# Transposes by halves of rows, VectorE's statistics behind the first projection, and band copies shared between ScalarE and VectorE

## The chip, the cores and the metric

The kernel runs on one core of a Trainium2 chip. The metric is the device time of one execution in microseconds, given as the median of the runs shown. TensorE multiplies and transposes into PSUM, which has eight banks of 512 fp32 columns in this kernel's use. VectorE and ScalarE empty PSUM, GpSimd (POOL in the profile) works in SBUF, and SyncE's queue (SP) issues nearly all DMAs.

## The reference

Two layers of the same form work on an image `x` of 512 x 512 positions with 64 channels. `_gn` normalises `x` over groups of two channels and all positions. Then, with DIM 64, HID 128 and WIN 4:

```python
xn = _ln(x, norm_scale, norm_bias)
left  = (xn @ Wl + bl) * mask * sigmoid(xn @ Wlg + blg)
right = (xn @ Wr + br) * mask * sigmoid(xn @ Wrg + brg)
out_gate = sigmoid(xn @ Wog + bog)
out = _banded_ingoing(left, right, WIN)   # out[i, j] = sum over k, |k - i| <= 4, of left[k, i] * right[k, j]
out = _ln(out, out_norm_scale, out_norm_bias) * out_gate
return out @ Wo + bo
# x = x + layer0(_gn(x)); x = x + layer1(_gn(x))
```

Everything is fp32. The band sum is, for each hidden channel, a product of a banded matrix of `left` with `right`.

## The kernel before

Rows of the image are cut into nine overlapping blocks of 64. Columns are taken in two halves of 256, and both halves lie above one another on the 128 partitions: partitions 0 to 63 hold the block's rows for columns of the first half, 64 to 127 the same rows for the second. A **unit** is 8 columns of both halves (`JU = 8`), 128 x 512 numbers; 16 units make a **chunk** of 128 columns, and each layer has 18 chunks, so 288 units and 288 outputs.

The work is staged over steps `t` in `layer`, and every instruction inside it keeps the order in which it is written (`InOrder`, line 355; the trace puts all of them at line 362). One step works on several units of different age:

- `load`, then `affine` on GpSimd (the group normalisation: `z` times `ga`, plus `gb`), `inner_stats` on VectorE (`sti`), and `inner_norm` on GpSimd (`z` minus mean, times `rs`).
- `transposed` (line 430): four TensorE transposes of 128 x 128 from `z` into one bank, one ScalarE instruction into `zT`, and a DMA of `zT` to `later`.
- `right` (line 459), twice per unit: four products into a pair of banks, a sigmoid on ScalarE into `sg`, and a product on VectorE into `RO`. `left` is alike and runs only in the first few steps.
- `mix` (line 511): sixteen products of the band matrix `A` with `RO` into a pair of banks, copied back to `RO` by halves. A chunk's 16 mixes lie in ten of 16 steps: 2, 1, 2, 2, 1, 2, 1, 2, 2, 1; the other six have none.
- `out_stats` on VectorE (`sto`), `norm` on ScalarE (eight instructions into `on`), both on mixed columns.
- `recall` fetches `zT` again as `zg`; `gates` (line 594) multiplies it by the gate weights and takes the sigmoid into `gate`; `turned` (line 613) transposes `on` into two banks, and VectorE multiplies each by its gate into `ZH`.
- `fetch` loads the old `x` into `XR`, `biased` adds a bias on GpSimd, `end` multiplies `ZH` by `Wo`, adds on VectorE, and stores. In the first layer `sums` gathers the next group normalisation's sums on TensorE.
- `solve`, every fourth step: a few VectorE instructions (`var`, `nm`, `rs`) and the inverse square root on GpSimd for four steps' statistics.

On TensorE a step runs: gates, right, right, transposes of `z`, `turned`, `end`, `sums`, mixes. Outputs run 30 steps behind the units; between them lie the first steps without outputs, and at the end of a layer steps without units.

PSUM is dealt out by two pools: `one_bank` (three buffers in the first layer, where `acc` takes the eighth bank, four in the second) and `two_banks` (two buffers of a pair). A buffer is given again only when all its readers are done. `right` and `mix` take pairs; gates, transposes and `end` take single banks.

The copies of `mix` are shared so:

```python
            if on_scalar[n]:
                en.scalar.copy(o, v)
            else:
                en.vector.tensor_copy(o, v)
...
                mix(c, A[c, h0 // HA], h0, [True, n + 1 < len(mixes[t])])
```

so that of a step's last mix the first half goes to ScalarE and the second to VectorE, and of an earlier one in that step both halves go to ScalarE.

Of the kernel before, what the change touches and what calls it, by code (L numbers as in the profile page):

```python
# [8 lines left out]
F32 = mybir.dt.float32  # L9
I32 = mybir.dt.int32  # L10
AF = mybir.ActivationFunctionType
ALU = mybir.AluOpType
# [67 lines left out]
def tile_two_banded_layers(  # L80
# [47 lines left out]
    def one_bank():  # L128
        return ps.tile([P, 512], F32, tag="ps", name="bank")
# [290 lines left out]
    def inner_stats(u: Unit, st: bass.AP, k: int):  # L420

        en.vector.bn_stats(st[:, k, :], u.z[:, 2 * k : 2 * k + 2, :].rearrange("p t c -> p c t"))
# [6 lines left out]

    def transposed(u: Unit):  # L430

        u.t = ztp.tile([P, JU // 2, P], F32, tag="zT", name="zT")
        pt = one_bank()
        for k in range(JU // 2):
            en.tensor.transpose(
                pt[:, k * P : (k + 1) * P],
                u.z[:, 2 * k : 2 * k + 2, :].rearrange("p j c -> p (j c)"), ident,
            )
        en.scalar.activation(u.t.rearrange("c k p -> c (k p)"), pt, AF.Identity, bias=1.0)
        if u.near is None:  # L440
            en.sync.dma_start(later[u.at], u.t)

    def place(k: int, e: int) -> int:

        return k // 2 * 4 + 2 * e + k % 2
# [62 lines left out]
            )  # L508
        return A

    def mix(c: int, A: bass.AP, h0: int, on_scalar: list):


        j0 = c % 2 * (JC - JW)
        R = RO[:, :, j0 : j0 + JC, :]
        pb = two_banks()
        ph = pb.rearrange("i (h j) -> i h j", j=JC)
        for turn in range(2):
            for h in range(HB // 2):
                for e in range(2):  # L520
                    part = slice(e * S, (e + 1) * S)
                    hh = (turn ^ e) * (HB // 2) + h
                    en.tensor.matmul(
                        ph[part, hh, :], lhsT=A[part, :, h0 % HA + hh],
                        rhs=R[part, (h0 + hh) // 2, :, hh % 2],
                        start=True, stop=True,
                    )
        q = HB // 4
        for n in range(2):
            o = R[:, h0 // 2 + n * q : h0 // 2 + (n + 1) * q]  # L530
            v = pb.rearrange("i (h t j) -> i h j t", t=2, j=JC)[:, n * q : (n + 1) * q]
            if on_scalar[n]:
                en.scalar.copy(o, v)
            else:
                en.vector.tensor_copy(o, v)
# [54 lines left out]
    def recall(o: Out):  # L590
        o.t = ztg.tile([P, JU // 2, P], F32, tag="zg", name="zg")
        en.sync.dma_start(o.t, later[o.at])

    def gates(o: Out, w: dict):
        b = o.blk
        o.g = []
        pgs = [
            one_bank()[:, : 2 * JQ * b.m].rearrange("h (k p) -> h k p", p=b.m) for e in range(2)
        ]
        for e, pg in enumerate(pgs):  # L600
            part = slice(e * D, (e + 1) * D)
            en.tensor.matmul(
                pg, lhsT=w["gate"][part],
                rhs=o.t[part].rearrange("c k (e p) -> c (k e) p", e=2)[:, :, b.lo : b.hi],
                start=True, stop=True,
            )
        for pg in pgs:
            g = gp.tile([H, 2 * JQ * (S - WIN)], F32, tag="gate", name="gate")
            g = g[:, : 2 * JQ * b.m].rearrange("h (k p) -> h k p", p=b.m)
            en.scalar.activation(g, pg, AF.Sigmoid)  # L610
            o.g.append(g)

    def turned(o: Out, w: dict):

        b = o.blk
        for e in range(2):
            pt = one_bank()
            for k in range(JQ):
                en.tensor.transpose(
                    pt[:, k * P : (k + 1) * P], o.on[:, place(k, e), :], ident  # L620
                )
            zh = ZH[(2 * o.n + e) % len(ZH)]
            en.vector.scalar_tensor_tensor(
                zh[:, :, : b.m], pt.rearrange("h (k p) -> h k p", p=S)[:, :, b.lo : b.hi], w["ob"], o.g[e],
                ALU.add, ALU.mult,
            )

    def rows_of(v: bass.AP, o: Out, e: int):
# [14 lines left out]
    def end(dst: bass.AP, o: Out, w: dict):  # L643
        m = o.blk.m
        po = one_bank().rearrange("i (j c) -> i j c", c=D)
        for k in range(JQ):
            for e in range(2):
                for n in range(2):

                    en.tensor.matmul(  # L650
                        po[n * S : (n + 1) * S, 2 * k + e, :],
                        lhsT=ZH[(2 * o.n + e) % len(ZH)][:, 2 * k + n, :], rhs=w["Wo"],
                        start=True, stop=True,
                    )
        f = o.xr[: S + m, :, 1 : 1 + 2 * D]
        en.vector.tensor_tensor(
            f, po[: S + m].rearrange("i (k t) c -> i k (t c)", t=2), f, ALU.add
        )
        for e in range(2):
            en.sync.dma_start(rows_of(dst, o, e), o.xr[e * S : e * S + m, :, 1 : 1 + 2 * D])  # L660
# [13 lines left out]
    def layer(src: bass.AP, dst: bass.AP, w: dict, stats: bool, then=None):  # L674
# [56 lines left out]
        for t in range(min(loads), last_t + 3):  # L731
            if then and t == max(units) + 2:
                then()
            for u in loads.get(t, []):
                if u not in early:
                    load(src, u)
            if t + 2 in outs:
                recall(outs[t + 2])
            if t + 1 in outs:
                fetch(src, outs[t + 1], w, t + 1)  # L740
            for c, h in slabs.get(t, []):
                A[c, h] = take_left(c // per, h)

            for o in looks.get(t, []):
                if sto is None:
                    sto = sm.tile([P, NB // 2, 6], F32, tag="sto", name="sto"), []
                st, os = sto
                for k in range(JU // 2):
                    out_stats(o, st[:, len(os) * (JU // 2) :], k)
                os.append(o)  # L750

            for u in affines.pop(t, []):
                affine(u, en.vector if u.at < NU + 4 else en.gpsimd)
            if t % 4 == 3 and t > NU:
                then_affine = affines.pop(t + 1, [])
            if t in outs:
                gates(outs[t], w)

            todo = []
            for at, u in inners.get(t, []):  # L760
                key = (at + 2) // 4
                if key not in sti:
                    sti[key] = sm.tile([P, 3 * NB // 4, 6], F32, tag="sti", name="sti", bufs=3), []
                st, us = sti[key]
                n = len(us) * (JU // 2)
                u.mean = st[:, n : n + JU // 2, 1::3]
                todo += [(u, st[:, n : n + JU // 2, :], k) for k in range(JU // 2)]
                us.append(u)
            for v in todo[: len(todo) // 2]:
                inner_stats(*v)  # L770
            if t in units:
                for q in range(0, JU, JQ):
                    right(units[t], q, w)
            if t in lefts:
                for q in range(0, min(JU, NEAR * JQ - lefts[t].near), JQ):
                    left(lefts[t], q, w)
            for u in inputs(t + 2):
                inner_norm(u)
            for u in inputs(t + 1):
                transposed(u)  # L780
            if t in outs:
                turned(outs[t], w)
                biased(outs[t], w, stats)
            for v in todo[len(todo) // 2 :]:
                inner_stats(*v)
            if t - 1 in outs:
                end(dst, outs[t - 1], w)
            if stats and t - 2 in outs:
                sums(outs[t - 2], t - 2 == first_t, t - 2 == last_t)
            if t % 4 == 3:  # L790
                st, us = sti.pop((t + 5) // 4, (None, []))
                so, os = sto or (None, [])
                sto = None
                for u in then_affine:
                    affine(u, en.gpsimd)
                then_affine = []
                if us or os:
                    solve(w, us, os, st, so)
            if t + 1 in outs:
                norm(outs[t + 1])  # L800
            for n, (c, h0) in enumerate(mixes.get(t, [])):
                mix(c, A[c, h0 // HA], h0, [True, n + 1 < len(mixes[t])])

    class Slices:

# [84 lines left out]
    lp = ctx.enter_context(tc.tile_pool(name="lp", bufs=NA))  # L890
    wk = ctx.enter_context(tc.tile_pool(name="wk", bufs=3))
    onp = ctx.enter_context(tc.tile_pool(name="onp", bufs=1))
    gp = ctx.enter_context(tc.tile_pool(name="gp", bufs=2))

    next(one, None)
    nc.sync.dma_start(pack, spare)
# [35 lines left out]
```

## Time and profile before

| | |
|---|---|
| Median of 3 runs | 5073.46 us (5070.14 to 5074.28) |
| The profiled execution's own time | 5074.14 us, span 5072.3 us |
| TensorE matmul busy | 4496.1 us, 89% of the span |
| GpSimd, ScalarE, VectorE busy | 3826.9, 3793.8, 3732.8 us |
| Granted TensorE clock | 0.978 over the span, 1.0 in the steady stretches |
| One chunk of 16 steps, steady | 124.9 us (first layer), 121.1 us (second) |

Busy time is the union of an engine's instructions; idle time of an engine that nobody waits for costs nothing. In the timeline each line is a run of like instructions on one engine: start, length, engine, operation, `out<-in`, sizes and count; a bracket tells the idle time ahead of it and what ended it. fp32 products appear in the trace as two instructions each, transposes as one. The last row of the table is taken from the starts of the gate products in the trace.

### The profile page before, as it was taken

To read this page: it belongs to the slowest core of one execution; us is meant where nothing else is said; L and a number is where in the kernel's file an instruction comes from. 1 tells how busy PE (TensorE), PEld (TensorE's weight loads), DVE (VectorE), ACT (ScalarE), POOL (GpSimd) and SP (SyncE) were. 2 spreads that over 40 slices of the span, in tenths; PEclk is the share of its full clock that TensorE was granted. 3 is DMA by queue.
4 is the path that set the end of the run, shared out by engine and by line. 5 is a ranking of instruction groups with operands and counts; after the bars stand their busy time and mean duration, and the time that the engine had idled before them with its cause. 6 is when DMAs were issued, how large, how long until landed. Compare 5 with 4: busy or idle time off the path is not lost.

```text
span 5072.3 us, 159784 instructions
## 1 busy us (share of the span) xinstructions
PE 4496.1 (89%) x60138; PEld 3714.8 (73%) x60138; DVE 3732.8 (74%) x9445; ACT 3793.8 (75%) x8328; POOL 3826.9 (75%) x4739
## 2 busy tenths in 40 slices
PE   1027999999999999999995599999999999999999
PEld 0015788888888888888873478888888888888886
DVE  6764677777777777777766467777777777777776
ACT  0013788888888888888884268888888888888888
POOL 0037888888888888888733598888888888888863
PEclk9988999999999999999997799999999999999999
DMA  7924666666666666666663456767676776777766
GB/s 317 400 58 125 176 194 197 195 195 193 198 196 195 194 194 197 196 194 198 189 171 102 106 176 201 202 198 202 200 205 201 202 203 200 202 204 204 204 182 173
DMA packets 905291, 981.45 MB, mean 193 GB/s; under 512 B 114210, under 2 KB 641608, under 8 KB 900168
## 3 DMA queue, kind: packets, MB, share of 16 engines
q1 hardware_dynamic: 897248, 948.49, 63.5%
q10 hardware_dynamic: 7272, 22.73, 1.1%
q8 instruction: 477, 7.82, 0.7%
q14 instruction: 294, 2.41, 0.2%
HBM read 658.42 MB, written 312.46 MB: 191 GB/s over the span
## 4 chain that ended last, share of the span: by engine, by line
PE 72%; POOL 9%; DMA 6%; DVE 4%; ACT 3%; issue 2%; SPq 2%; another core or an unknown queue 0%; ACTq 0%; POOLq 0%; DVEq 0%
PE banks L362 38%; PE bank L362 32%; POOL z L362 6%; ACT on L362 2%; DMA left_of<-nothing 2%; PE acc L362 2%; SPq L362 2%; DVE RO L362 1%; POOL XR L362 1%; DMA gn_x<-in_x_dram 1%; POOL rsqrt L362 1%; DVE ZH L362 1%; DMA XR<-mid_x 1%; DVE sto L362 1%; ACT gate L362 1%
## 5 line engine op out<-in xcount | busy, mean ns | idle before, releaser
L362 ACT ACTIVATE on<-RO,nm,rs 128x128 f32<-128x128 f32 x4608 | 1879.2, 495 | 172.4 <-PE bank L362 169.9
L362 PE MATMUL banks<-pack,zT 64*128 64x256 f32 x9360 | 1213.1, 389 | 137.0 <-ACT zT L362 76.6
L362 PEld LDWEIGHTS banks<-pack,zT 64*128 64x128 f32 x9360 | 967.2, 192 | 419.8 <-issue 180.4
L362 PE MATMUL banks<-RO,A 64*64 64x128 f32 x18432 | 1154.5, 277 | 15.6 <-DVE RO L362 15.4
L362 PEld LDWEIGHTS banks<-RO,A 64*64 64x64 f32 x18432 | 1082.4, 183 | 43.6 <-DVE RO L362 18.6
L362 DVE TENSOR_TENSOR RO<-banks,sg 128x512 f32<-128x512 f32 x1152 | 747.0, 681 | 258.8 <-ACT sg L362 258.0
L362 ACT ACTIVATE sg<-banks 128x512 f32<-128x512 f32 (+1 forms) x1188 | 682.7, 589 | 319.8 <-PE banks L362 208.0
L362 DVE COPY RO<-banks 128x512 f32<-128x512 f32 x360 | 248.9, 692 | 869.1 <-ACT RO L362 869.1
L362 DVE BATCH_NORM_STATS2 sto<-RO 128x6 f32<-128x256 f32 x2304 | 797.5, 411 | 1.2
L362 DVE SCALAR_TENSOR_TENSOR ZH<-bank,pack,gate 128x448 f32<-128x448 f32 (+1 forms) x1152 | 740.0, 682 | 37.6 <-ACT gate L362 36.3
L362 POOL TENSOR_TENSOR z<-z,gb 128x512 f32<-128x512 f32 x536 | 687.7, 1283 | 42.1
L362 POOL TENSOR_TENSOR z<-z,ga 128x512 f32<-128x512 f32 x536 | 687.5, 1283 | 0.1
L362 PE MATMUL bank<-zg,pack 64*128 64x448 f32 (+1 forms) x2304 | 657.4, 595 | 18.9 <-DVE ZH L362 15.8
L362 PE MATMUL bank<-pack,ZH 128*64 128x64 f32 x18432 | 663.5, 225 | 2.8 <-ACT zT L362 0.3
L362 ACT ACTIVATE gate<-bank 128x448 f32<-128x448 f32 (+1 forms) x1152 | 567.1, 542 | 126.6 <-PE bank L362 125.8
L362 PEld LDWEIGHTS bank<-pack,ZH 128*64 128x64 f32 x18432 | 584.0, 138 | 100.3 <-ACT zT L362 83.2
L362 POOL TENSOR_TENSOR z<-z,rs 128x512 f32<-128x512 f32 x586 | 618.0, 1055 | 45.9
L362 PE MATMUL bank<-ident,on 128*128 128x128 f32 x4608 | 616.6, 274 | 14.7 <-ACT gate L362 12.1
L362 POOL TENSOR_TENSOR z<-z,sti 128x512 f32<-128x512 f32 x586 | 623.8, 1065 | 0.0
L362 ACT COPY RO<-banks 128x512 f32<-128x512 f32 x792 | 441.2, 586 | 239.0 <-PE banks L362 237.8
L362 PEld LDWEIGHTS bank<-ident,on 128*128 128x128 f32 x4608 | 519.7, 141 | 74.0 <-ACT on L362 24.3
L362 POOL TENSOR_TENSOR XR<-XR,pack 120x512 f32<-120x512 f32 (+1 forms) x352 | 418.4, 1189 | 192.4 <-DMA XR<-mid_x 90.4
(137 smaller groups left out, 3927.6 us busy)
## 6 DMA issues: line engine op xcount, KB each, us to landing
later<-zT SPq DMA_DIRECT2D x576, 256.0 KB
A<-left_of SPq DMA_DIRECT2D x576, 256.0 KB
zg<-later SPq DMA_DIRECT2D x576, 256.0 KB
z<-in_x_dram SPq DMA_DIRECT2D x576, 128.0 KB
z<-mid_x SPq DMA_DIRECT2D x576, 128.0 KB
gn_x<-in_x_dram SPq DMA_DIRECT2D x16, 4096.0 KB
XR<-in_x_dram SPq DMA_DIRECT2D x448, 112.0 KB
mid_x<-XR SPq DMA_DIRECT2D x448, 112.0 KB
```

Of the source, the lines that this page charges most:

```text
L362: return lambda *a, **k: tc.keep_in_program_order(f(*a, **k))
```

## The change

1. Each transpose of 128 rows becomes two of 64 rows, each with its 64 x 64 part of the identity, and the two write to different banks. This holds for `z` and for `on`. In the steady state the two halves of `z` take one pair of `two_banks`; the first 17 units and the lefts take two single banks. The copy to `zT` moves to `kept`.
2. In `turned` the two banks are now the two halves of rows, both held at once; `gates` writes both sigmoids to one tile (`gp` has one buffer for two), and `ZH` is indexed accordingly in `end`.
3. The step's order: `recall` goes behind `fetch` and `take_left`; `out_stats` are split in three places (`looking[:3]` first, two behind the first `right`, the rest behind `turned`); gates go behind the first `right`; `turned` goes ahead of the transposes of `z`; all `inner_stats` go behind `turned`.
4. Every mix has its first half copied by ScalarE and its second by VectorE.

```diff
     def transposed(u: Unit):
+        if u.near is None and u.at > NU:
+            u.pt = [two_banks().rearrange("c (n x) -> c n x", n=2)[:, :, : JU // 2 * S]]
+            halves = [u.pt[0][:, n] for n in range(2)]
+        else:
+            halves = [one_bank()[:, : JU // 2 * S] for n in range(2)]
+            u.pt = [h.unsqueeze(1) for h in halves]
+        for k in range(JU // 2):
+            for n in range(2):
+                part = slice(n * S, (n + 1) * S)
+                en.tensor.transpose(
+                    halves[n][:, k * S : (k + 1) * S],
+                    u.z[part, 2 * k : 2 * k + 2, :].rearrange("p j c -> p (j c)"),
+                    ident[part, part],
+                )
+
+    def kept(u: Unit):
         u.t = ztp.tile([P, JU // 2, P], F32, tag="zT", name="zT")
-        pt = one_bank()
-        for k in range(JU // 2):
-            en.tensor.transpose(
-                pt[:, k * P : (k + 1) * P],
-                u.z[:, 2 * k : 2 * k + 2, :].rearrange("p j c -> p (j c)"), ident,
-            )
-        en.scalar.activation(u.t.rearrange("c k p -> c (k p)"), pt, AF.Identity, bias=1.0)
+        to = u.t.rearrange("c k (n p) -> c n k p", n=2)
+        for n, pt in enumerate(u.pt):
+            en.scalar.activation(
+                to[:, n : n + pt.shape[1]], pt.rearrange("c n (k p) -> c n k p", p=S),
+                AF.Identity, bias=1.0,
+            )
...
-            if on_scalar[n]:
+            if n == 0:
                 en.scalar.copy(o, v)
...
     def turned(o: Out, w: dict):
         b = o.blk
+        pts = [one_bank().rearrange("h (x p) -> h x p", p=S) for n in range(2)]
         for e in range(2):
-            pt = one_bank()
             for k in range(JQ):
-                en.tensor.transpose(
-                    pt[:, k * P : (k + 1) * P], o.on[:, place(k, e), :], ident
-                )
-            zh = ZH[(2 * o.n + e) % len(ZH)]
+                for n, pt in enumerate(pts):
+                    part = slice(n * S, (n + 1) * S)
+                    en.tensor.transpose(
+                        pt[:, e * JQ + k, :], o.on[part, place(k, e), :], ident[part, part]
+                    )
+        for n, pt in enumerate(pts):
             en.vector.scalar_tensor_tensor(
-                zh[:, :, : b.m], pt.rearrange("h (k p) -> h k p", p=S)[:, :, b.lo : b.hi], w["ob"], o.g[e],
-                ALU.add, ALU.mult,
+                ZH[(2 * o.n + n) % len(ZH)][:, :, : b.m], pt[:, :, b.lo : b.hi], w["ob"],
+                o.g[:, n], ALU.add, ALU.mult,
             )
...
-            if t + 2 in outs:
-                recall(outs[t + 2])
             if t + 1 in outs:
                 fetch(src, outs[t + 1], w, t + 1)
             for c, h in slabs.get(t, []):
                 A[c, h] = take_left(c // per, h)
-
+            if t + 2 in outs:
+                recall(outs[t + 2])
...
+            for v in looking[:3]:
+                out_stats(*v)
...
-            if t in outs:
-                gates(outs[t], w)
...
-            for v in todo[: len(todo) // 2]:
-                inner_stats(*v)
             if t in units:
-                for q in range(0, JU, JQ):
-                    right(units[t], q, w)
+                right(units[t], 0, w)
+            for v in looking[3:5]:
+                out_stats(*v)
+            if t in outs:
+                gates(outs[t], w)
+            if t in units:
+                right(units[t], JQ, w)
...
+            if t in outs:
+                turned(outs[t], w)
             for u in inputs(t + 1):
                 transposed(u)
+                kept(u)
             if t in outs:
-                turned(outs[t], w)
                 biased(outs[t], w, stats)
-            for v in todo[len(todo) // 2 :]:
+            for v in looking[5:]:
+                out_stats(*v)
+            for v in todo:
                 inner_stats(*v)
...
-                mix(c, A[c, h0 // HA], h0, [True, n + 1 < len(mixes[t])])
+                mix(c, A[c, h0 // HA], h0)
```

More of the change, by code (lines that the diff above doesn't have):

```diff
@@ L509, in take_left, with mix @@
         return A
-    def mix(c: int, A: bass.AP, h0: int, on_scalar: list):
+    def mix(c: int, A: bass.AP, h0: int):
         j0 = c % 2 * (JC - JW)
@@ L595, in gates @@
         b = o.blk
[L596 to L599, printed above, removed]
+        n = 2 * JQ * b.m
+        pgs = [one_bank()[:, :n].rearrange("h (k p) -> h k p", p=b.m) for e in range(2)]
         for e, pg in enumerate(pgs):
@@ L606, in gates @@
             )
[L607 to L611, printed above, removed]
+        g = gp.tile([H, 4 * JQ * (S - WIN)], F32, tag="gate", name="gate")
+        for e, pg in enumerate(pgs):
+            en.scalar.activation(
+                g[:, e * n : (e + 1) * n].rearrange("h (k p) -> h k p", p=b.m), pg, AF.Sigmoid
+            )
+        o.g = g[:, : 2 * n].rearrange("h (x n p) -> h n x p", n=2, p=b.m)
     def turned(o: Out, w: dict):
         b = o.blk
+        pts = [one_bank().rearrange("h (x p) -> h x p", p=S) for n in range(2)]
         for e in range(2):
-            pt = one_bank()
             for k in range(JQ):
-                en.tensor.transpose(
-                    pt[:, k * P : (k + 1) * P], o.on[:, place(k, e), :], ident
-                )
-            zh = ZH[(2 * o.n + e) % len(ZH)]
+                for n, pt in enumerate(pts):
[4 more added lines that the diff above has]
+        for n, pt in enumerate(pts):
             en.vector.scalar_tensor_tensor(
-                zh[:, :, : b.m], pt.rearrange("h (k p) -> h k p", p=S)[:, :, b.lo : b.hi], w["ob"], o.g[e],
-                ALU.add, ALU.mult,
+                ZH[(2 * o.n + n) % len(ZH)][:, :, : b.m], pt[:, :, b.lo : b.hi], w["ob"],
+                o.g[:, n], ALU.add, ALU.mult,
             )
@@ L651, in end @@
                         po[n * S : (n + 1) * S, 2 * k + e, :],
-                        lhsT=ZH[(2 * o.n + e) % len(ZH)][:, 2 * k + n, :], rhs=w["Wo"],
+                        lhsT=ZH[(2 * o.n + n) % len(ZH)][:, e * JQ + k, :], rhs=w["Wo"],
                         start=True, stop=True,
@@ L742, in layer @@
                 A[c, h] = take_left(c // per, h)
+            if t + 2 in outs:
+                recall(outs[t + 2])
+            looking = []
             for o in looks.get(t, []):
@@ L747, in layer @@
                 st, os = sto
-                for k in range(JU // 2):
-                    out_stats(o, st[:, len(os) * (JU // 2) :], k)
+                n = len(os) * (JU // 2)
+                looking += [(o, st[:, n : n + JU // 2, :], k) for k in range(JU // 2)]
                 os.append(o)
+            for v in looking[:3]:
+                out_stats(*v)
             for u in affines.pop(t, []):
@@ L892, in tile_two_banded_layers @@
     onp = ctx.enter_context(tc.tile_pool(name="onp", bufs=1))
-    gp = ctx.enter_context(tc.tile_pool(name="gp", bufs=2))
+    gp = ctx.enter_context(tc.tile_pool(name="gp", bufs=1))
     next(one, None)
```

## The prediction

> **What bounds it now.** I read the page's busy shares first, then the chain that ended last, then the timeline of one step.
>
> ```profile
> PE 4496.1 (89%) x60138; PEld 3714.8 (73%) x60138; DVE 3732.8 (74%) x9445; ACT 3793.8 (75%) x8328; POOL 3826.9 (75%) x4739
> ...
> PE 72%; POOL 9%; DMA 6%; DVE 4%; ACT 3%; issue 2%; SPq 2%; another core or an unknown queue 0%; ACTq 0%; POOLq 0%; DVEq 0%
> ```
>
> TensorE carries the chain; no other engine is near it. But a share is a mean over unlike steps, so here is one step of layer 2 that has two mixes (TensorE's timeline: start us, length us):
>
> ```profile
> 3256.31 3.94 PE L362 MATMUL banks<-RO,A 64*64 64x128 f32 x64
> 3260.18 1.02 PE L362 MATMUL bank<-zg,pack 64*128 64x448 f32 x4
> 3261.03 1.89 PE L362 MATMUL banks<-pack,zT 64*128 64x256 f32 x16
> 3262.86 0.66 PE L362 MATMUL bank<-ident,z 128*128 128x128 f32 x4
> 3263.35 1.04 PE L362 MATMUL bank<-ident,on 128*128 128x128 f32 x8
> 3264.32 1.15 PE L362 MATMUL bank<-pack,ZH 128*64 128x64 f32 x32
> 3265.40 3.94 PE L362 MATMUL banks<-RO,A 64*64 64x128 f32 x64
> ```
>
> Gate to next gate is 9.09 us, without a bracket (idle). Over the whole trace, steps of layer 2 take 9.09 with two mixes and 7.26 with one; layer 1, which also runs `sums`, 9.56 and 7.73. All of these are TensorE alone. The six steps of a chunk without a mix take 6.5 down to 5.88, mostly bound elsewhere: 5.88 is what POOL needs for affine (2.6), `inner_norm` (2.1) and XR (1.2), and there TensorE shows idle brackets "<-POOL z". Hence a gain on TensorE counts in ten steps of sixteen.
>
> VectorE in the same step (same columns; a bracket is the idle time before the line and who ended it). It carries little slack where `solve` falls:
>
> ```profile
> 3260.92 0.69 DVE L362 COPY RO<-banks 128x512 f32<-128x512 f32 x1 [3.25 <-ACT RO L362]
> 3261.53 1.39 DVE L362 BATCH_NORM_STATS2 sto<-RO 128x6 f32<-128x256 f32 x4
> 3262.84 0.87 DVE L362 BATCH_NORM_STATS2 sti<-z 128x6 f32<-128x128 f32 x4
> 3263.63 1.27 DVE L362 TENSOR_TENSOR RO<-banks,sg 128x512 f32<-128x512 f32 x2
> 3264.82 1.26 DVE L362 SCALAR_TENSOR_TENSOR ZH<-bank,pack,gate 128x448 f32<-128x448 f32 x2
> 3266.00 0.88 DVE L362 BATCH_NORM_STATS2 sti<-z 128x6 f32<-128x128 f32 x4
> 3266.80 0.67 DVE L362 TENSOR_TENSOR XR<-bank,XR 120x512 f32<-120x512 f32 x1
> ...
> 3267.70 1.15 DVE L362 TENSOR_SCALAR var<-var 128x32 f32<-128x32 f32 x1
> ...
> 3270.01 0.69 DVE L362 COPY RO<-banks 128x512 f32<-128x512 f32 x1 [0.93 <-ACT RO L362]
> ```
>
> Of 9.09 us VectorE idles 0.93 in this heaviest step (eight input statistics and a `solve`), and 3.25 in the one before.
>
> **What the Trainium skill says.** "TensorE: Matmul & The Clock Gate", Part 3: matmuls and weight loads overlap where their row groups differ. The trace agrees: the projection's products on rows 0-63 and 64-127 start 7 ns apart, a pair every 216 ns. "TensorEngine Tiling (Array Packing)", Key Properties: changing the tiling mode drains TensorE. It shows: from the projection's last pair to the second transpose is 479 ns, where 216 + 109 would be the bare pace, so 154 lost. Its Gotcha 1 says row tiles must write different banks; the new code gives each half its own.
>
> **Transposes.** Now 12 per step (4 of z, 8 of `on`), one every 109 ns in the steady run. After: 24 with 64 rows and 64 columns moving, alternating row groups. No transpose on half the rows is in the trace. Nearest is the output product in `end`, also 64 moving columns, two at a time: in the trace's single instructions a pair starts every 58 ns, with its two weight loads. From below: a whole transpose's unhidden weight load costs about 56 ns (first of the z group 329 ns against 273), so two concurrent loads fit 58. From above: 107 a pair, if loads take the 104 ns seen unhidden in the gates' products (first pair 640 ns, second 536); worse, if halves do not overlap, 24 x 58. I take 58: 12 x 109 = 1.31 becomes 0.70, less 0.61. The order is now projection, `turned`, z, `end`: the mode change ahead of the transposes goes (0.15), that after them stays. **-0.76 us a step.** Steps with mixes, units and outputs together: ten per chunk, 16 chunks, two layers = 320. 320 x 0.76 = **-243 us**. Mixless steps: nothing, since POOL's 5.88 stands and ScalarE's 5.8 (gates 0.95, sigmoids 1.06, zT 0.53, eight of `on` 3.24) is hardly less. The ramps, where only units or only outputs run, are not TensorE's either: the page's slices show it 0 to 7 tenths busy there; nothing.
>
> **Copies.** Per chunk six of 22 half-copies leave ScalarE (0.56 each) for VectorE (0.61 spacing): 216 in all, 120 us off ScalarE, 132 onto VectorE. ScalarE was idle in those steps, so its relief is worth nothing. VectorE's cost lies in a bank. `transposed` now takes a pair from `two_banks`, which has two, so in a two-mix step (right, right, z, mix, mix) the next step's first `right` needs the first mix's pair. Formerly ScalarE emptied it alone. Now VectorE's half comes behind everything in its queue.
>
> From the step's start, TensorE reaches that `right` at 8.3. VectorE: last step's copy waits for ScalarE's half and ends at 1.3; three statistics 2.3; first RO 2.9; one statistic 3.25. The second RO waits for the second sigmoid, which follows the gates: product ends 2.7, sigmoid 3.45, RO 4.1. ZH 5.3, input statistics 6.1, XR 6.7, copy 7.3: in time by 1.0. In the two `solve` steps with eight input statistics add 0.8 and 0.9 to 2.0 (the `var` line above): 9.0 to 10.1, late by 0.7 to 1.8. I take 1.2. In layer 1 TensorE's step is 0.47 longer, so 0.7. 16 x 2 x (1.2 + 0.7) = **+61 us**. Bounds: 0, if VectorE enters ahead; about 9 us a chunk, if every two-mix step is late.
>
> **Order.** Statistics behind the first product are the same instructions, counted above. z's pair needs the first RO (2.9) before 3.1: no wait, but no room. Gates behind the first `right`, and one gate tile instead of two: the tile was read by ZH at 5.3 of the step before; nothing. `turned` holds two banks at once, and both ZH wait for all sixteen halves, 0.2 us later, inside VectorE's wait for the sigmoid. On SP `recall` moves behind the fetch's two issues and up to two of A (0.86 and 1.09 us a pair), so zg starts at most 2 us later; it is wanted by the gates two steps on, over 12 us, and these now come 0.9 us later in their step: nothing. Nothing else waits for SP there, since z and XR are now ahead of it. POOL's queue keeps its order and its work. z's one ScalarE read keeps its 512 elements (0.60); only the first units and lefts split in two, under 10 us of ScalarE in a stretch bound by POOL.
>
> Sum: -243 + 61 = -182. The profiled execution took 5074.1 (span 5072.3 and 1.8 around it), 0.7 above the median: 4892 against it, **4891 us** against the median.
>
> **Rivals.**
> - Weight loads on half rows bind: 107 a pair. Then the transposes gain 0.02, the mode change 0.15: 320 x 0.17 = 54, less about 30 of waiting at the slower pace: 5050. For it: the 104 ns in the gates. Against: that load is for a product that goes in two passes of instructions; transposes go in one.
> - The halves don't overlap (the change doesn't do what it says): 1.39 for 1.31, so 0.07 gained a step, 22 us, less 40 of bank waits: 5090. Against: the 7 ns pairs.
> - **Slower: VectorE's copy holds TensorE through the pair of banks.** It decides where the wait passes 7.6 us a chunk (ten times 0.76). Six two-mix steps at 1 us and two `solve` steps 1.5 more make 9: 1.4 x 32 = +45, 5118. For it: margins of 1.0 and 0.2 us. Against: VectorE's sum over a chunk is 94.9 + 3.7 of some 115 us, and a single-mix step takes one pair fewer, so its next `right` needs only z's pair, emptied by ScalarE long before.
>
> **Numbers.** Main case (4800 to 4980) 0.70; weight loads 0.09; no overlap 0.05; bank wait 0.14; the rest, near no change, 0.02. No wait at all gives 5073 - 243 = 4830, and some mixless gain (0.3 us of ScalarE's wait on `on` in 96 steps, 29 us) 4801. The range 4795 to 5100 takes that in and the first two rivals; the main case alone is 4800 to 4980. A measurement here tells 0.2% (10 us) from no change. Faster: main case and weight loads, 0.79. No overlap lies on the edge and is halved: same 0.02 + 0.02 = 0.04, slower 0.14 + 0.03 = 0.17.
>
> **What would show it.** Right: pairs of `ident` rows 7 ns apart and a pair about each 58 ns; two-mix steps at about 8.3 (layer 2) and 8.8 (layer 1); TensorE idle "<-DVE RO" ahead of the first projection after the `solve` steps; VectorE copies at 576. Wrong: halves spaced 50 ns or more singly, or "DVE RO" waits of 1 us in every two-mix step.

## The result, and the profile after

The changed kernel takes 5032.66 us (median of 4 runs, 5025.97 to 5036.56), the kernel before, on the same chip, 5073.87 us (5070.14 to 5079.49). The ratio is 0.9916, 95% interval 0.9899 to 0.9934: faster by 41 us, where 182 were forecast. The profiled execution spans 5031.9 us against 5072.3.

From the page of the kernel after, busy time and share of the span, and the start of the chain that ended last:

```profile
PE 4211.9 (84%) x67090; PEld 3564.2 (71%) x67090; DVE 3875.7 (77%) x9661; ACT 3636.6 (72%) x8156; POOL 3827.9 (76%) x4739
...
PE 3%; ACT 2%; DVE 1%; POOL 0%; issue 0%; DMA 0%; SPq 0%; ACTq 0%; DVEq 0%; POOLq 0%
```

TensorE's busy time fell by 284 us, its span by 40: its idle time grew from 576 to 820 us. The chain was followed over only 6% of the span here, so it says nothing on the steady stretches; they have to be read step by step. A two-mix step of layer 2, in TensorE's timeline:

```profile
3265.25 0.92 PE L362 MATMUL bank<-zg,pack 64*128 64x448 f32 x4
3266.01 1.03 PE L362 MATMUL banks<-pack,zT 64*128 64x256 f32 x8
3266.87 0.66 PE L362 MATMUL bank<-ident,on 64*128 64x64 f32 x16
3267.36 0.42 PE L362 MATMUL banks<-ident,z 64*128 64x64 f32 x8
3267.71 1.15 PE L362 MATMUL bank<-pack,ZH 128*64 128x64 f32 x32
3268.79 3.94 PE L362 MATMUL banks<-RO,A 64*64 64x128 f32 x64
3272.81 1.13 PE L362 MATMUL banks<-pack,zT 64*128 64x256 f32 x8
```

Sixteen halves of `on` take 0.49 us from their start to that of the next line, where eight whole transposes took 0.97. Gate to next gate (3265.25 to 3273.78) is 8.53 us against 9.09. So the transposes cost what was forecast. This step is one of the undisturbed ones. The largest loss shows once per chunk. This is the same view some 50 us later, in the first step with mixes after six without:

```profile
3317.76 0.66 PE L362 MATMUL bank<-ident,on 64*128 64x64 f32 x16
3322.27 0.69 PE L362 MATMUL banks<-ident,z 64*128 64x64 f32 x8 [3.85 <-POOL rsqrt L362]
3322.89 1.97 PE L362 MATMUL bank<-pack,ZH 128*64 128x64 f32 x32
3324.79 5.17 PE L362 MATMUL banks<-RO,A 64*64 64x128 f32 x64
```

TensorE stands for 3.85 us ahead of z's transposes, and then `end` and the mixes take 1.97 and 5.17 us instead of 1.15 and 3.94. The bracket names GpSimd, but its last work on the `z` that is transposed here, `inner_norm`, had ended by 3316.6. z's pair comes from `two_banks`, whose two pairs hold this step's two projections, so z waits for the first product into `RO`. VectorE's timeline of the same stretch has it as its last line:

```profile
3317.37 0.46 DVE L362 TENSOR_SCALAR var<-sti 128x32 f32<-128x32 f32 x1
3317.75 1.32 DVE L362 SCALAR_TENSOR_TENSOR var<-sto,pack 128x32 f32<-128x32 f32 x1
3319.10 0.18 DVE L362 TENSOR_SCALAR var<-var 128x32 f32<-128x32 f32 x1
3319.19 1.25 DVE L362 TENSOR_SCALAR nm<-sto 128x32 f32<-128x32 f32 x1
3320.36 0.18 DVE L362 TENSOR_SCALAR rs<-var 128x64 int32<-128x64 int32 x1
3320.46 1.07 DVE L362 BATCH_NORM_STATS2 sto<-RO 128x6 f32<-128x256 f32 x3
3321.45 0.67 DVE L362 TENSOR_TENSOR RO<-banks,sg 128x512 f32<-128x512 f32 x1
```

The product ends at 3322.12 and z starts at 3322.27. Ahead of it lie the whole `solve` of the step before and the three statistics `looking[:3]`. GpSimd's `rsqrt` merely happened to end beside it. And the `solve` is slow: five instructions take 3.17 us, two of them over 1.2. GpSimd's timeline shows what runs meanwhile:

```profile
3317.74 1.28 POOL L362 TENSOR_TENSOR z<-z,ga 128x512 f32<-128x512 f32 x1
3319.10 1.30 POOL L362 TENSOR_TENSOR z<-z,gb 128x512 f32<-128x512 f32 x1
```

Each slow instruction of VectorE starts within 0.1 us of one of `affine` and ends within 0.1 us of its end.

Mean step lengths over the first 16 chunks of each layer, from the starts of the gate products, place the loss. Steps of a chunk are called m0 to m15: m0 to m9 have mixes (m0 two), m10 to m15 none, and `solve` falls into m3, m7, m11 and m15.

| us, layer 1 / layer 2 | m0 | m1 to m9 | m10 to m15 | chunk |
|---|---|---|---|---|
| before | 9.78 / 10.12 | 78.8 / 74.5 | 36.5 / 36.0 | 125.0 / 120.7 |
| after | 13.03 / 13.65 | 73.3 / 71.3 | 35.6 / 35.5 | 121.9 / 120.5 |

Single m0 of the kernel after lie between 10.3 and 15.5 us; the one shown, 14.7, is among the longer ones.

### The profile page after: what moved, and what is told of

It reads as the page before. It is cut to its first block, busy times and chain, and to the rows that moved or that the text cites. A ratio compares the mean times of both kernels' runs of the same rounds, so it can differ in the third digit from the quotient of the medians.

```text
span 5031.9 us, 173294 instructions
## 1 busy us (share of the span) xinstructions
PE 4211.9 (84%) x67090; PEld 3564.2 (71%) x67090; DVE 3875.7 (77%) x9661; ACT 3636.6 (72%) x8156; POOL 3827.9 (76%) x4739
## 5 line engine op out<-in xcount | busy, mean ns | idle before, releaser
L362 PE MATMUL banks<-pack,zT 64*128 64x256 f32 x9360 | 1322.6, 404 | 128.9 <-ACT zT L362 56.2
L362 PEld LDWEIGHTS banks<-pack,zT 64*128 64x128 f32 x9360 | 884.9, 194 | 493.7 <-DVE RO L362 200.8
L362 DVE TENSOR_TENSOR RO<-banks,sg 128x512 f32<-128x512 f32 x1152 | 787.8, 684 | 347.6 <-ACT sg L362 331.5
L362 DVE COPY RO<-banks 128x512 f32<-128x512 f32 x576 | 397.9, 691 | 592.8 <-ACT RO L362 592.8
L362 DVE BATCH_NORM_STATS2 sto<-RO 128x6 f32<-128x256 f32 x2304 | 847.1, 414 | 1.2
L362 PE MATMUL bank<-pack,ZH 128*64 128x64 f32 x18432 | 689.4, 230 | 5.6 <-ACT gate L362 5.2
L362 PE MATMUL bank<-zg,pack 64*128 64x448 f32 (+1 forms) x2304 | 551.7, 550 | 1.2 <-DMA zg<-later 0.8
L362 ACT COPY RO<-banks 128x512 f32<-128x512 f32 x576 | 335.7, 583 | 299.2 <-PE banks L362 299.2
L362 PEld LDWEIGHTS bank<-ident,on 64*128 64x128 f32 x9216 | 402.6, 139 | 210.1 <-ACT gate L362 97.2
L362 PE MATMUL bank<-ident,on 64*128 64x64 f32 x9216 | 443.2, 225 | 86.3 <-ACT gate L362 59.3
```

Source lines behind the costliest of these rows:

```text
L362: return lambda *a, **k: tc.keep_in_program_order(f(*a, **k))
```

## The experiments

Three theories stood at the start. **A**: z's pair waits for the first `RO` product behind VectorE's `solve`, and the fall of TensorE's clock makes it dearer. **B**: VectorE has too many copies. **C**: GpSimd's work sets a floor for a chunk. Times are medians; ratios are to the kernel before, run beside each.

### Solve, copies, and the parts of the change

**solve_late**: the kernel after, with each `solve` held back behind the next step's projections.

```diff
                 if us or os:
-                    solve(w, us, os, st, so)
+                    due = us, os, st, so
...
+            if due:
+                solve(w, *due)
+                due = None
             for u in inputs(t + 2):
                 inner_norm(u)
```

> The changed kernel, but solve of a fourth step is written after the next step's two right products instead of ahead of them, so VectorE's var, nm and rs come behind both RO products. Theory A (the first mix step of a chunk loses its time because z's pair of banks waits for the first RO product, which queues behind solve, and then the tensor clock drops): that step falls from 13 to 15 us to 9 to 10, a chunk of layer 2 from 121 to about 117, total 4890 to 4940. Theory B (VectorE has too many copies): the order within VectorE does not matter, total 5020 to 5040. Theory C (GpSimd's work is the floor of a chunk): the chunk stays at 119 to 121, total above 5000.

5066.4 us, 0.9994 (0.9985 to 1.0003): the gain is gone. Yet m0 fell to 9.59 / 9.63, the step that theory A names. The time came back in m5 (10.35 / 10.66, from 9.01 / 9.18) and m13 (9.37 / 9.64, from 5.68 / 5.14). Waits of TensorE, layer 2 (total, times, longest):

```profile
PE banks L362 <- POOL z L362: 63.0, 29, 3.5
```

Here the wait is for a late `z`: the statistics come a step later to GpSimd, and `inner_norm` with them; in m5 and m13 of layer 2 it ends 0.05 us before z's transposes start. So the `solve` ahead of m0 is part of the cause there, but not every `solve` can be moved.

**copies_old**: after, with the earlier sharing of the copies.

```diff
-            if n == 0:
+            if on_scalar[n]:
                 en.scalar.copy(o, v)
...
-                mix(c, A[c, h0 // HA], h0)
+                mix(c, A[c, h0 // HA], h0, [True, n + 1 < len(mixes[t])])
```

> The changed kernel with the band copies shared as before (22 half-copies of a chunk on ScalarE, 10 on VectorE). Theory A: the first mix step of a chunk keeps its 13 to 15 us; only the other two-mix steps of layer 2 go from 9.2 to 8.5, total 4975 to 5010. Theory B: that step goes to 9 to 10 us too and the total to about 4900. Theory C: total unchanged at 5020 to 5040.

5013.45 us, 0.989 (0.9875 to 0.9904): 19 us better than after by the medians, with intervals that just overlap. m0 stays at 13.15 / 12.93. In layer 2 m3 goes from 8.91 to 8.49, m7 from 9.25 to 9.01; layer 1 doesn't change. The copies cost a little, and are not the loss: B falls as the main cause.

**zwhole**: after, but z transposed whole into one bank of `one_bank`; `on` still in halves.

```diff
-        if u.near is None and u.at > NU:
-            u.pt = [two_banks().rearrange("c (n x) -> c n x", n=2)[:, :, : JU // 2 * S]]
...
+        u.pt = one_bank()
+        for k in range(JU // 2):
+            en.tensor.transpose(
+                u.pt[:, k * P : (k + 1) * P],
+                u.z[:, 2 * k : 2 * k + 2, :].rearrange("p j c -> p (j c)"), ident,
+            )
```

> The changed kernel with z transposed whole again (four of 128 rows, into one single bank, read by ScalarE at once); on stays in halves. z no longer takes a pair of banks. Costs TensorE 0.24 us and one more mode change of 0.15 us a step. Theory A: TensorE's idle <-DVE RO ahead of z is gone, the first mix step is at 9 to 10 us, the others 0.4 us longer, total 5000 to 5040. Theory B: no wait is won, the 0.4 us in 320 steps come on top, total 5130 to 5160. Theory C: total 5020 to 5060.

5212.09 us, 1.0278 (1.0262 to 1.0293). m0 is 10.55 / 10.13, so the pair is what makes m0 wait. But layer 1 takes 134.2 a chunk, from 121.9, so the total lies far over the 5000 to 5040 that theory A gave. **order_only**, after with z and `on` whole, two gate tiles and the earlier copies, so that hardly more than the step's order is left, shows the same:

```diff
-        pts = [one_bank().rearrange("h (x p) -> h x p", p=S) for n in range(2)]
         for e in range(2):
+            pt = one_bank()
             for k in range(JQ):
```

> The changed kernel's step order alone (statistics and gates behind the first right product, turned ahead of z's transposes), with whole transposes into single banks and the copies shared as before. Theory A and B: TensorE has the same work, its mode changes one more, so nothing is won: 5070 to 5110. Theory C: layer 2 near the same 119 to 121 us a chunk; layer 1 is TensorE's and its three single banks: total 5060 to 5150.

5241.71 us, 1.0334 (1.0316 to 1.0351), layer 1 again 134.2. Waits of TensorE in 1000 to 2200 us, of zwhole and then of order_only:

```profile
PE bank L362 <- DVE ZH L362: 146.2, 144, 1.3
```

```profile
PE bank L362 <- DVE ZH L362: 96.7, 144, 1.0
```

At 8.4 us a step, 144 waits are one in each: `turned`, z and `end` follow one another on three single banks, and `end` waits for `ZH` to empty one. Moving z to a pair removes this.

**halves_only**: before, with the transposes by halves alone (points 1 and 2 of the change); order and copies as before. The lines show where `kept` then stands.

```diff
             for u in inputs(t + 1):
                 transposed(u)
+                kept(u)
```

> The kernel before with the transposes by halves of rows alone (z's halves in a pair of banks, on's in two single banks, one gate tile); the step's order and the copies are those of before. Theory A: z stands directly behind the second right product, so it waits for the first RO product in more steps than in the changed kernel; the gain is smaller or gone, total 5030 to 5120. Theory B: without the extra copies the halves bring most of their price, total 4880 to 4950. Theory C: total 5020 to 5060.

5458.14 us, 1.0761 (1.0745 to 1.0777). TensorE now waits for `RO` in most steps, not in m0 alone (in layer 2, 3100 to 4700: 144 waits of 195.8 us in all, 136 of them ahead of z, in some 190 steps). TensorE's timeline, with z's halves directly behind the second projection:

```profile
3256.07 0.47 PE L362 MATMUL banks<-ident,z 64*128 64x64 f32 x8 [1.58 <-DVE RO L362]
```

So the halves need the order, and the order needs z's move to a pair; each alone is slower than the kernel before.

### GpSimd

**before_nobias** and **after_nobias** take `biased` (1.2 us of GpSimd a step) out of each kernel.

```diff
-        n = S + o.blk.m
-        f = o.xr[:n, :, 1 : 1 + 2 * D]
-        add = fewer if stats and o.blk.m < S - WIN else w["add"]
-        en.gpsimd.tensor_tensor(f, f, mid(add[:n], JU // 2), ALU.add)
+        pass
```

> The kernel before without biased: GpSimd does not add the output's bias to XR, so 576 of its instructions of 1.19 us (about 19 us a chunk) are left out. Theory C (GpSimd, which needs 7.03 us a step with its short gaps, is the floor): the mix steps of before are TensorE's and stay at 9.09 and 7.26, only the mixless ones shrink, a chunk by 3 to 5 us, total 4920 to 4990. Theory A (VectorE's queue in front of z's pair of banks): GpSimd matters little, total 5040 to 5070.

5044.59 us, 0.995 (0.9935 to 0.9965).

> The changed kernel without biased, as in before_nobias. Theory C: the floor is lifted and the change gives its price: a chunk at 112 to 116 us, total 4780 to 4850, and 120 to 200 us under before_nobias. Theory A: the first mix step of a chunk stays at 12 us and more, since VectorE's solve still stands ahead of the first RO product; total 4960 to 5020, and 50 us or less under before_nobias.

4931.42 us, 0.9726 (0.9711 to 0.974). The relief is worth about 27 us before and 101 after. Both kernels leave the bias out. m0 falls to 9.93 / 10.18, and `solve` on VectorE takes 0.72 us, where the mean was 1.30. C in its bare form falls, for the time saved is at m0 and not spread over the steps; but a GpSimd without lead is what puts `affine` beside `solve`.

**affine_behind**: after, with `affine` behind `solve` in GpSimd's queue.

```diff
-                for u in then_affine:
-                    affine(u, en.gpsimd)
-                then_affine = []
                 if us or os:
                     solve(w, us, os, st, so)
+                for u in then_affine:
+                    affine(u, en.gpsimd)
+                then_affine = []
```

> The changed kernel with GpSimd's affine of the next step written behind solve instead of ahead of it, so GpSimd is idle while VectorE does solve and the two don't meet. Theory A: VectorE's var and nm of the last mixless step fall from 1.3 us to 0.2, the first mix step by 2 to 3 us, total 4930 to 4970. Theory C: the rest that GpSimd takes while it waits for rs is added to a floor, total 5040 to 5120, although the var lines are short.

5033.23 us, 0.9925 (0.9911 to 0.994), as after. `solve` shortens to 0.93 us and m0 to 10.35 / 11.11; m13 rises to 7.86 / 7.00, from 5.68 / 5.14. The overlap is part of the cause of m0; that queue's order gives the gain back where GpSimd has no room.

### A longer solve

In the next four the inverse square root runs on VectorE, which lengthens each of 160 `solve` (four a chunk, and those of the ramps) by about 2.5 us there and frees GpSimd: **root_on_vector** (after), **root_copies** (after, earlier copies), **before_root** (before), **root_late** (root_copies, every `solve` held back as in solve_late).

```diff
-        rsqrt(r, v, en.vector, en.gpsimd)
+        rsqrt(r, v, en.vector, en.vector)
```

> The changed kernel with the ten steps of the inverse square root in solve on VectorE instead of GpSimd: nothing is left out, GpSimd is relieved of about 1 us a step, and rs is there some 2 us sooner; VectorE gets about 1.5 us every fourth step. If GpSimd's lack of lead is the cause, this acts as leaving biased out did: the first mix step at 9.8 to 10.5 us, total 4890 to 4950. If VectorE's queue ahead of the first RO product is the cause by itself, that step gets longer still: total 5040 to 5090.

5421.18 us, 1.0691 (1.0675 to 1.0707): 389 us over after, 2.4 per `solve`. Not all of it is VectorE's own time: in the steady stretches (1000 to 2200 and 3100 to 4700 us) TensorE ran at half clock for 324 us, against 119 in the kernel after, which makes some 100 of the 389 (an estimate: half of the difference).

> As root_on_vector, with the band copies shared as before the change (six half-copies a chunk back on ScalarE). VectorE then has room for the square roots: in both theories faster than root_on_vector, by 15 to 40 us; total 4860 to 4930.

5281.15 us, 1.0413 (1.0397 to 1.0428). The earlier copies give 140 us here, where 15 to 40 were expected: they weigh more when VectorE has more to do at `solve`.

> The kernel before with the inverse square root on VectorE. Its mix steps are TensorE's and stay at 9.57, 7.73, 9.10 and 7.26; only mixless steps and the first mix step of layer 2 can shrink: total 5030 to 5060 if GpSimd is the cause of the lost gain; the changed kernel then gains 100 us or more on this one. If VectorE is short, 5070 to 5100.

5183.43 us, 1.0221 (1.0206 to 1.0236): only 2.2%, some 0.7 us per `solve`, in the kernel before.

> As root_copies, with solve behind the next step's right products. The first mix step then waits neither for solve nor, with rs soon ready, for z: 9 to 9.6 us, and the waits that solve_late had in two other steps (1.4 and 3 us) are mostly gone since nothing on GpSimd lies between: total 4830 to 4890. If they stay, 4900 to 4960.

5041.48 us, 0.9942 (0.9925 to 0.9958): with every `solve` out of the way, the root on VectorE ends 28 us over copies_old. No run holds `solve` back with the earlier copies and the root on GpSimd, so these 28 are not its price alone. VectorE's time at `solve` is on the path for the larger part in the kernel after, and was so for under a third in the kernel before. In root_on_vector the first projection behind an m3 shows the wait that the prediction had priced:

```profile
3321.71 1.13 PE L362 MATMUL banks<-pack,zT 64*128 64x256 f32 x8 [2.90 <-DVE RO L362]
```

### One solve moved

Only the `solve` of m15 stands ahead of an m0. **late15** holds that one back alone; **before_late15** does so in the kernel before; **late15_copies** adds the earlier copies; **late15_copies_nobias** drops `biased` as well.

```diff
-                if us or os:
+                if (us or os) and t % 16 == 15:
+                    due = us, os, st, so
+                elif us or os:
                     solve(w, us, os, st, so)
```

> The changed kernel with one of the four solves of a chunk, that of the last mixless step (t % 16 == 15), behind the next step's right products. If the first mix step's wait behind VectorE's solve is time by itself: that step at 9.6 us for 13.0 and 13.7, no other step longer, 34 chunks x 3.5 = 115 us less: total 4905 to 4945. If GpSimd's work is the floor that returns it: another step grows by as much, total 5000 to 5040.

5018.59 us, 0.9905 (0.9888 to 0.9922), not told apart from after. m0 is 9.59 / 9.61 at last, but m3 is now 10.86 / 10.75 (from 9.04 / 8.91) and m7 in layer 2 10.18 (from 9.25). At the end of an m3:

```profile
3338.35 1.14 PE L362 MATMUL banks<-pack,zT 64*128 64x256 f32 x8 [2.30 <-DVE RO L362]
```

That is VectorE's copy, late behind the `solve` of m3: the wait that the prediction put there. This `solve` takes 2.5 / 2.6 us, and 0.8 in the kernel after. In VectorE's timeline of late15 two of its instructions are slow, one beside `biased`, one beside `affine`:

```profile
3335.38 1.05 DVE L362 TENSOR_SCALAR var<-var 128x32 f32<-128x32 f32 x1
3336.46 1.23 DVE L362 TENSOR_SCALAR rs<-var 128x64 int32<-128x64 int32 x1
```

In an m3 of the kernel after, GpSimd had finished both early and stood waiting for that `solve`:

```profile
3353.95 0.29 POOL L362 TENSOR_TENSOR rsqrt<-rs 128x64 f32<-128x64 f32 x1 [2.64 <-DVE rs L362]
```

So m0's stall had hidden the wait of m3: while TensorE stood, GpSimd caught up. That fits after_nobias, where GpSimd is relieved: m0 is near 10 there too, the `solve` of m3 takes 0.72, and m3 stays at 8.97 / 8.85. The total lies where theory C had put it, 5000 to 5040, and another step grew, as it said; but the earlier copies take most of this wait away (in late15_copies, below, m3 is 8.96 / 8.50 and m4 rises by 0.5 to 1.0), so it is no floor.

> The kernel before with that one solve moved. There z takes a single bank and does not wait for RO; only the first mix step of layer 2 waits for VectorE (10.1 for 9.1). Both: at most 1 us in 16 chunks, total 5050 to 5075.

5086.69 us, 1.0033 (1.0022 to 1.0045): the move by itself costs 0.3%. None of that is in the 32 chunks of the table, which take 2 us less; it lies in the ramps, which late15 pays for as well.

> As late15, with the band copies shared as before. If the wait is time by itself, 20 us under late15: 4885 to 4925. If GpSimd is the floor: 4990 to 5020.

**4940.15 us** (4935.07 to 4941.09), 0.9743 (0.9729 to 0.9758). It leaves nothing out and beats both kernels: 128 us under before, and 92 under after by the medians, where the two edits singly give 14 and 19. A chunk takes 119.0 / 116.5. The time lies above the 4885 to 4925 expected if the wait is time by itself, and far under the 4990 expected if GpSimd is the floor. In TensorE's timeline the wait of an m0 is now

```profile
3273.59 0.46 PE L362 MATMUL banks<-ident,z 64*128 64x64 f32 x8 [0.87 <-DVE RO L362]
```

and its busy line

```profile
PE 4176.5 (85%) x67090; PEld 3522.3 (71%) x67090; DVE 3761.0 (76%) x9445; ACT 3739.3 (76%) x8372; POOL 3821.3 (77%) x4739
```

has ScalarE 103 us above after and VectorE 115 below: the copies are back where there was room.

> As late15_copies, without biased, so that GpSimd lacks 19 us a chunk. If VectorE's queue was the cause, little is left for GpSimd: 4860 to 4910, 30 us or less under late15_copies. If GpSimd is the floor, 80 us or more under it.

4913.97 us, 0.9694 (0.9679 to 0.9708). With m0 mended, GpSimd's relief is worth 26 us, no longer 100.

## Why the prediction was wrong in size

**The price of the transposes held.** A pair every 58 ns was assumed, and the halves of `on` show 0.49 us for eight pairs, 61 ns. In the step shown, `on` and z take 0.84 us to the start of `end`, from 1.46: 0.62 less, where 0.61 was named. Gates and projections ahead of them take 0.09 less, where 0.15 was named for the mode change. Single-mix steps of layer 2 went from 7.26 to 6.54, which is 0.72 against 0.76. Undisturbed two-mix steps reach 8.5 and, in layer 1, 9.0, where 8.3 and 8.8 were named; in layer 2 the difference is the next projection, which starts 4.02 us behind the first product of the mixes, from 3.87, and with the earlier copies m8 takes 8.38. Weight loads don't bind, and halves overlap: those two rivals are out.

Layer 1 keeps some 0.15 us a step for another reason. In most of m1 to m9 the halves of `on` take 0.55 to 0.60 us there and those of z 0.39, where undisturbed ones in layer 2 take 0.49 and 0.35. The single banks are the likely cause, but in m1 to m9 the waits are too short for the list; those that it has lie in m0 and in mixless steps (TensorE's waits, 1000 to 2200 us):

```profile
PE bank L362 <- ACT gate L362: 18.4, 44, 0.5
```

`turned` takes two banks at once, and one of them must first be emptied by the gate's sigmoid. The prediction had named the two banks and priced them at nothing.

**The step that failed** is "z's pair needs the first RO (2.9) before 3.1: no wait, but no room". The 2.9 was read from a step between steps with mixes. It doesn't hold for m0, where VectorE enters late behind six steps in which GpSimd sets the pace, a `solve` and three statistics. The prediction took 0.76 from all ten steps with mixes, m0 too. m0 grew by 3.25 / 3.53 instead, so it missed by 4.01 and 4.29, or 16 x 8.30 = 133 us. On the mean some 3.1 / 3.6 us of an m0 are the wait, and most of the rest is the slower clock behind it. late15 and zwhole show that both parts are needed: take the m15 `solve` or the pair away, and m0 is near 10. The total gives no hint of this: 5033 lies inside the range on record, and near the 5050 of the rival with weight loads, by coincidence.

**The +61 was in the wrong place.** For m3 and m7 it forecast 1.4 us a chunk in layer 1 and 2.4 in layer 2. m1 to m9 together changed by -5.44 and -3.24, where nine times -0.76 plus these waits make -5.44 and -4.44. In layer 1 the sum fits by luck: m3 waits for VectorE only 0.1 us, and most of the 1.4 is the slower halves of `on` and z (0.95). In layer 2 the 1.20 us lost make 19 us. There the two-mix steps m2, m5 and m7 take 9.2 and m8 8.5: they follow single-mix steps, and "a single-mix step takes one pair fewer, so its next `right` needs only z's pair" failed. After right, right, z, mix the next step's first projection takes z's pair and starts at once, but its second takes the mix's, which has just been filled. In the trace of such an m7 it starts 1.06 us behind the gates, in the m8 shown 0.76; z's halves start 0.70 behind those of `on`, against 0.49. With the earlier copies m2, m5 and m7 still take 9.0, so VectorE's half is only a part of it. That the +61 mechanism itself is real, and larger, late15 shows: with m0 mended, m3 and m7 together rise by 1.9 us a chunk in layer 1 and 2.8 in layer 2.

**Mixless steps** were put at nothing, and gave 0.92 and 0.51 a chunk, 23 us. What lies outside these 32 chunks, also put at nothing, cost 13 us, 9 of them ahead of layer 1's first m0. The cause of these 9 was not tried. The sum closes: 133 + 19 - 23 + 13 = 142, and 182 less the 40 by which the span fell is 142.

**POOL's queue "keeps its order and its work"** is true, and missed the point: GpSimd is busy 1408.8 us of the 1600 from 3100 to 4700 (1410.7 before), without lead when the mixes begin. That decides how long VectorE's `solve` takes: the mean was 1.54 us before and 1.30 after, against 0.72 without `biased`. The one ahead of m0 takes 2.5 / 3.0 us before and 2.8 after, so it is not its length that is new, but that z's bank hangs on it. The prediction's own line of a 1.15 us `var`, among neighbours of 0.2, was the sign, in a kernel where nothing hung on it.

**The rival** "VectorE's copy holds TensorE through the pair of banks" was near the mechanism: the pair, VectorE's queue, `solve`. But it was not the copy that was late, and not in every two-mix step; its 5118 didn't come. `recall`, moved behind the fetch, cost next to nothing: the page puts 0.8 us in all on waits for `zg`.

## What to carry to other kernels

When an edit moves a tile to a pool with fewer buffers, list who must empty each buffer and what stands in that engine's queue then, in every kind of step, the first after a change of regime above all; a margin read from a steady step says nothing there. Where one stall ends another's wait, repairs don't add: singly they gave 14 and 19 us, which is hardly told from nothing, together 92. A short instruction that takes six times its usual length is a lead, even where it costs nothing yet.

## What the hardware showed beyond that

- **TensorE's clock.** In the steady stretches (1000 to 2200 and 3100 to 4700 us) the kernel before never ran at half clock; the kernel after did for 30.7 and 88.7 us, always in pieces of 3.41 us or twice that. The Trainium skill, "TensorE: Matmul & The Clock Gate", Part 1, gives a free-running window of about 3.4 us and a half-rate clock after an idle one. The pieces agree. A wholly idle window isn't needed here. Cut into windows of 3.41 us in step with these pieces, the two stretches of the kernel after hold 785 such windows at full clock. In 27 of them TensorE was busy for 51% or less, and half clock followed every one; it followed none of the 744 that were busy for over 60%, and 3 of the 14 between. In five other runs of this case the border lies between 44% and 61%. In the m0 shown, `end` and the mixes lost 0.82 + 1.23 = 2.05 us to it, so the wait's price was 3.85 plus half as much again. Windows around two waits of 0.43 and 1.60 us in an m12, and in that m0 (start:end, length, busy time of PE, PEld, DVE, ACT, POOL, then the granted clock):

```profile
3293.46:3296.87 3.41, 1.38 (x28) 0.96 (x24) 3.38 (x13) 2.07 (x5) 1.66 (x5) 1.00 0.59 182
3296.87:3300.28 3.41, 3.41 (x44) 2.99 (x42) 2.89 (x7) 3.26 (x9) 2.84 (x9) 0.50 0.73 234
3317.35:3320.76 3.41, 1.07 (x22) 0.83 (x18) 3.38 (x7) 2.41 (x6) 3.11 (x4) 1.00 0.78 249
3320.76:3324.17 3.41, 1.90 (x32) 1.82 (x34) 3.41 (x8) 1.17 (x3) 2.72 (x9) 0.50 0.76 224
```

- **VectorE beside GpSimd.** The small instructions of `solve` take 0.15 to 0.21 us alone. In the kernel after, all 31 of `nm` and of the last `var` that started 0.09 to 0.37 us into one of GpSimd's `affine` took 1.1 to 1.3 us and ended with it; 17 that started within 6 ns of its start took 0.18. "GPSIMD Engine Reference", Specifications, says that the SBUF interfaces are shared and that VectorE's instructions with two SBUF inputs, or in a two-port mode, contend. The trace agrees for the `var` with two inputs; whether `nm` and the last `var`, with one, ran in such a mode it doesn't tell. VectorE's instruction isn't merely slowed here: it lasts until GpSimd's ends. Statistics beside GpSimd kept their lengths (1.07 us for three).
